# Layer two's norm folded into its matrices, ScalarE evictions, products in steps, and edge lists made in node order in a two-layer graph kernel

## The chip, the cores and the metric

The kernel runs on one core of a Trainium2 chip. The core has a matrix engine (TensorE, PE in the profile, with its weight loads as PEld), three engines for elementwise work (VectorE or DVE, ScalarE or ACT, GpSimd or POOL), a queue engine (SyncE or SP) and 16 DMA engines. Each engine runs its instructions in order, and they wait for each other through semaphores. Data lies in device memory (DRAM) or in on-chip memory of 128 partitions (SBUF), and matrix products land in PSUM. The metric is the device time of one execution in microseconds; lower is better.

## What is computed

There are N = 1250 nodes with 768 features, E = 20000 edges (source, destination, one of 34 types), sorted by destination. The reference, cut to what matters:

```
h   = relu(layernorm(x))
# layer one, 8 heads of 96; layer two, one head of 768
def gatv2(x, src, dst, Ws, bs, Wd, bd, attn):
    fs = x @ Ws + bs;  fd = x @ Wd + bd
    e  = leaky_relu(fs[src] + fd[dst], 0.2)
    logits = sum(e * attn)                       # per head
    alpha  = softmax of logits over the edges of a destination
    return elu(segment_sum(alpha * fs[src], dst))
g   = layernorm(gatv2(h, ..., W1s, b1s, W1d, b1d, attn1) + h) * ln1_w + ln1_b
o   = layernorm(gatv2(g, ..., Wos, bos, Wod, bod, attno)) * lno_w + lno_b
x   = x + o;  h = relu(layernorm(x))
# relational stage: mean of h over the edges of each type, times that type's 768 x 768 matrix
h1  = sum over r of mean_r(h[src]) @ W_rel[r] + h @ W_root + b_rgcn
out = x + normalised neighbour sum of (h1 @ W_gcn) + b_gcn
```

Everything is computed in 32-bit floats. A second path (`general_path`) stands behind a flag for inputs that don't fit the fast path's limits, and is not run here.

## The kernel before, in words

Nodes are ranked by in-degree and laid out as NT = 10 tiles of 128 nodes in that order. All nodes of tile k have at most CAPS[k] incoming edges (33, 22, 20, 18, 17, 16, 15, 14, 13, 11; 179 in all), so layer one and layer two each walk over 179 *slots*: slot s of tile k is the s-th incoming edge of each of the tile's 128 nodes.

**Front (`fast_front`, L627).** It loads the edges, x and layer one's weights, normalises x row by row (`h0`, also written to DRAM), turns it into columns, and finds for each node where its edges start and how many there are. From these come a key (L843 to L861: products into `wide`, copied to `keys`), the rank (ten passes of VectorE, L865), and a scatter of (node, first edge, degree) into `rank_d` in rank order (L880). The ranked record is read back (L901), and only then the edges of each ranked node are gathered as windows of 64 (L912) and shifted into place (L916 to L930). `sources(j)` (L807) computes node tile j of layer one's table `fs_d`: 26 products, two ScalarE copies, a store. Two of its ten calls stand between the steps of the ranking; `tc.issue_after` fixes that order on TensorE.

**Pair lists (`pairs`, L937, called from `prepare_lists`, L1349).** They give each edge its place in the lists by which the relational stage gathers. VectorE does nearly all of it, and three prefix sums go over TensorE (L966 to L983). The places are written to DRAM and read back (L1069, L1375), the lists are filled with default entries (L1354 to L1373), and each edge is then scattered into them, one indirect DMA for each slot.

**Layers one and two (`attention`, L1172).** The slots of a tile are cut into one or two chunks of at most CHUNK = 20. `front(c, i)` (L1194) issues for a slot an indirect gather of 128 rows of the table into `fs`, a ring of 24 buffers, and gives VectorE the logits: a maximum with the tile's negated destination rows (L1208), a product with the attention vector and a sum (L1213 and L1214 in layer one, L1210 in layer two). `softmax(c)` (L1217) turns a chunk's logits into weights. `back(c, i)` (L1250) scales the rows, on ScalarE by heads in layer one (L1266), and sums them on TensorE (L1268, L1258) into PSUM; the ring buffer is free after that. The loop at L1323 runs `back` of a chunk beside `front` of the next.

- `begin` (L1306) prepares the next tile's negated destination rows in the middle of a chunk. In layer one, `negated1` (L1409) gathers the tile's `h0` rows, makes columns and multiplies by W1d; VectorE evicts and applies the bias (L1416).
- `end` (L1282) closes a tile behind the loop over the chunk: shares, ELU, then `finish1` (L1420) or `finish2` (L1459). `finish1` adds h0, normalises, applies `lnw` and `lnb` (L1426, L1427), makes columns, multiplies by Wos, evicts with the bias (L1433), forms a further column of the table (L1435), scatters the 769 columns to layer two's table, multiplies by Wod and evicts the negated rows (L1440). Each product is one run of 24 instructions (`dense`, L1111).
- `list_edges` (L1385) puts the edge scatters into GpSimd's queue: 0.9 for each slot from slot 20 on, and 60, that is all the rest, behind layer one's last gather.

The products of a tile's start and end share one PSUM buffer (tag `mm2`) and one column buffer (`hT1`). The order on each engine is made by a planner that takes instructions by their place in the program and by a modelled time; `tc.issue_after(ins)` holds instructions of one engine behind `ins`.

**Relational stage and output (L1527, L1625).** 139 products of gathered tiles with the types' matrices, then the neighbour sums.

## Time and profile before

| | us |
|---|---|
| median of four runs | 2764.71 (2760.81 to 2769.98) |
| profiled execution, device time | 2764.21 |
| its span, first to last instruction | 2762.4 |
| first gather of layer one's rows | 154.3 |
| first scaling of gathered rows in layer one (L1266) | 246.7 |
| last gather of layer one | 794.1 |
| first gather of layer two | 886.5 |
| first load of a type's matrix | 1358.0 |
| granted TensorE clock, mean | 0.933 |

In the profile a row names the line of the program, the engine, the operation, what is written and what is read, how many instructions the row stands for, and in brackets how long the engine had been idle and what ended that. In a table by stage, busy times of the engines stand with the number of instructions in parentheses, then the granted clock, the share of the DMA engines and the rate in GB/s. A wait is given as total time, number of times and longest one. L1148 and L1152 are the helpers for indirect gathers and scatters, so their rows are told apart by what they write and read.

### The profile page before, as it was taken

Reading aid. Unit: us, or ns where it says so; the run is one execution under the profiler, and the core shown is the slowest. Engines: PE = TensorE matmul, PEld = TensorE weight load, DVE = VectorE, ACT = ScalarE, POOL = GpSimd, SP = SyncE. Lnnn points to the kernel's source line nnn. Section 1 sums busy time; section 2 is a strip of 40 time slices with the busy share of each in tenths; the row PEclk is TensorE's granted clock in tenths of the full one; section 3 lists DMA queues with packets and bytes.
Section 4 is the critical chain, followed back from the end, with each engine's and each line's share of the span. In section 5 each row is a group of like instructions: output and inputs, shape, how many; then the busy total and the mean of one; then the engine's idle time right before and its main releaser. Section 6 shows DMA issues by size and latency. Waiting matters only on the chain. (4 is left out here: it accounts for less than half of the span.)

```text
span 2762.4 us, 24188 instructions
## 1 busy us (share of the span) xinstructions
PE 2356.7 (85%) x7759; PEld 1366.4 (49%) x7759; DVE 1564.4 (57%) x2361; ACT 853.6 (31%) x2308; POOL 1525.2 (55%) x1113
## 2 busy tenths in 40 slices
PE   5953685789997486988699999999999999999688
PEld 3531252445454243544356666666666666666254
DVE  5599979998994999999262222222223222210262
ACT  3004765767862132333211121211211212212010
POOL 1343877777884775876275444444445454431471
PEclk9976897999999698999899999999999999999899
DMA  6155443445431776775477777777777777766783
GB/s 211 46 166 178 133 133 98 127 133 140 134 102 65 261 213 184 223 220 166 154 232 197 191 186 192 193 198 195 189 190 188 186 195 194 175 165 151 215 266 119
DMA packets 136548, 476.85 MB, mean 173 GB/s; under 512 B 26185, under 2 KB 28514, under 8 KB 136413
## 3 DMA queue, kind: packets, MB, share of 16 engines
q0 software_dynamic: 83712, 334.44, 46.7%
q1 hardware_dynamic: 48043, 134.21, 13.7%
q10 hardware_dynamic: 4658, 6.57, 0.7%
q8 instruction: 64, 1.05, 0.2%
q14 instruction: 71, 0.58, 0.1%
HBM read 385.91 MB, written 89.33 MB: 172 GB/s over the span
## 5 line engine op out<-in xcount | busy, mean ns | idle before, releaser
L1116 PE MATMUL ps<-wrel,mT 128*128 128x384 f32 x3336 | 1099.8, 486 | 1.0 <-DMA wrel<-in_L_gnn_W_rel_dram 1.0
L1116 PEld LDWEIGHTS ps<-wrel,mT 128*128 128x128 f32 x3336 | 623.5, 190 | 407.3 <-issue 1.4
L1148 POOL DMA_INDIRECT g<-r_h_d,lists x241 | 340.2, 1412 | 525.8 <-DVE g L1580 288.8
L1268 PE MATMUL ag<-fs,identf 128*128 128x384 f32 x716 | 288.4, 535 | 156.6 <-ACT fs L1266 146.9
L1580 DVE TENSOR_TENSOR g<-g,g 128x768 f32<-128x768 f32 x68 | 64.5, 949 | 614.8 <-DMA g<-r_h_d,lists 364.4
L1208 DVE TENSOR_TENSOR z<-fs,nfd 128x776 f32<-128x776 f32 (+1 forms) x358 | 347.5, 987 | 42.2 <-DMA fs<-f_fs_d,rec 21.2
L1266 ACT ACTIVATE fs<-fs,lg 128x96 f32<-128x96 f32 x1376 | 370.0, 363 | 0.3
L1258 PE MATMUL ag<-fs,dg 128*128 128x384 f32 x716 | 249.9, 510 | 82.6 <-ACT dg L1256 82.6
L1148 POOL DMA_INDIRECT fs<-f_fs_d,rec x179 | 247.3, 1382 | 97.4 <-issue 50.3
L1152 POOL DMA_INDIRECT r_pair_d<-rec,place x179 | 238.0, 1330 | 85.0 <-issue 43.9
L1603 POOL DMA_INDIRECT r_h_d<-y,lists x139 | 224.0, 1612 | 110.1 <-ACT y L1602 52.7
L1148 POOL DMA_INDIRECT fs<-r_fs_d,rec x179 | 239.4, 1337 | 81.1 <-issue 31.0
L1268 PEld LDWEIGHTS ag<-fs,identf 128*128 128x128 f32 x716 | 133.4, 202 | 298.4 <-ACT fs L1266 240.5
L1258 PEld LDWEIGHTS ag<-fs,dg 128*128 128x128 f32 x716 | 140.9, 200 | 188.5 <-ACT dg L1256 89.7
L1602 ACT ACTIVATE y<-ps,lists 128x768 f32<-128x768 f32 x71 | 64.1, 902 | 479.4 <-PE ps L1116 479.4
L1602 ACT ACTIVATE y<-ps,rcnt 128x768 f32<-128x768 f32 x68 | 61.4, 902 | 455.5 <-PE ps L1116 455.5
L1210 DVE SCALAR_TENSOR_TENSOR z<-z,attn_o 128x769 f32<-128x769 f32 x179 | 175.0, 995 | 0.6 <-ACT dg L1256 0.5
L1665 DVE TENSOR_TENSOR acc<-acc,nb 128x768 f32<-128x768 f32 x69 | 66.1, 958 | 187.0 <-DMA nb<-r_h_d,srcz 185.9
L1213 DVE TENSOR_TENSOR z<-z,attn 128x776 f32<-128x776 f32 x179 | 168.2, 954 | 0.1
L1214 DVE TENSOR_REDUCE lg<-z 128x8 f32<-128x776 f32 x179 | 167.8, 949 | 0.1
L1513 DVE SCALAR_TENSOR_TENSOR arow<-node,from_f,arow 128x1250 f16<-128x1250 f16 x110 | 166.2, 1511 | 1.7
L1104 PEld LDWEIGHTS pt<-identf,g 128*128 128x128 f32 x834 | 100.4, 142 | 54.6 <-issue 24.0
(283 smaller groups left out, 2314.3 us busy)
## 6 DMA issues: line engine op xcount, KB each, us to landing
wrel<-in_L_gnn_W_rel_dram SPq DMA_DIRECT2D x37, 2304.0 KB
g<-r_h_d,lists POOLq DMA_INDIRECT x241, 4.9
r_nfd_d<-fd SPq DMA_DIRECT2D x10, 384.0 KB
nfd<-r_nfd_d SPq DMA_DIRECT2D x10, 384.0 KB
r_x_d<-xb SPq DMA_DIRECT2D x10, 384.0 KB
x1r<-r_x_d SPq DMA_DIRECT2D x10, 384.0 KB
f_fs_d<-o_s SPq DMA_DIRECT2D x9, 388.0 KB
x<-in_x_dram SPq DMA_DIRECT2D x9, 384.0 KB
```

The costliest lines, as they stand in the source:

```text
L1116: last = nc.tensor.matmul(ps[:n, half, :f.HW], hT[:, k, j * P:j * P + n], w[:, k, cols], start=(k == 0), stop=(k == f.KC - 1 and not bias))
L1148: return nc.gpsimd.indirect_dma_start(out=to, out_offset=None, in_=table, in_offset=bass.IndirectOffsetOnAxis(ap=idx, axis=0))
L1152: s = nc.gpsimd.indirect_dma_start(out=table, out_offset=bass.IndirectOffsetOnAxis(ap=idx, axis=0), in_=rows, in_offset=None, **kw)
L1208: nc.vector.tensor_tensor(z, fs, t.nfd, op=ALU.max)
L1210: nc.vector.scalar_tensor_tensor(z[:, 0, :], z[:, 0, :], 1.0, attn_e[:, 0, :], op0=ALU.mult, op1=ALU.mult, accum_out=t.lg[:, s, :])
L1213: nc.vector.tensor_mul(z, z, attn_e)
L1214: nc.vector.tensor_reduce(t.lg[:, s, :], z, axis=AX.X, op=ALU.add)
L1258: nc.tensor.matmul(c.ps[:, half, :HW], dg, fs[:, 0, half * HW:(half + 1) * HW], start=begin, stop=end)
L1266: nc.scalar.activation(fs[:, h, :HD], fs[:, h, :HD], AF.Copy, scale=t.lg[:, s, h:h + 1])
L1268: nc.tensor.matmul(c.ps[:, half, :HW].rearrange("p (h d) -> p h d", d=HD), f.identf, fs[:, half * H // 2:(half + 1) * H // 2, :HD], start= ...
L1513: nc.vector.scalar_tensor_tensor(a, node16, from_f[:, k, s:s + 1], a, op0=ALU.is_equal, op1=ALU.add)
L1603: s = nc.gpsimd.indirect_dma_start(out=h1_d[:, :], out_offset=bass.IndirectOffsetOnAxis(ap=j.node, axis=0), in_=y, in_offset=None, compute ...
```

## The change

It has four parts.

*Front.* The edge windows are gathered and shifted in node order, before and beside the ranking, and the record that is scattered by rank carries a node's 33 edges with it (35 words instead of 4). None of the `sources` calls stands ahead of the ranking's products any more; all ten follow `last_keys`. The lists' default entries and zero rows are written in the front. `place` stays on the chip. Biases of layer one's destination rows are one row that a product with `ones_row` adds.

*Norm folded.* `ln1_w` is multiplied into Wos and Wod (`fold`, six ScalarE scalings each), `ln1_b` and the biases become one row for Wod and one row `bias_s`, which is added to layer two's weighted sums in `share`. The table's further column becomes a 769th column of Wos. Nodes without incoming edges are masked by `has`.

*Steps.* A tile's end and start return lists of steps: a transposition of three blocks, or six instructions of a product (half of one half). They go to `todo`, and the loop over a chunk runs them, spread evenly behind its slots. A tile with one chunk is closed two slots into the next chunk. ScalarE evicts each half of a product. For the last two tiles the product with Wos comes first, and that with Wod after both.

*Lists.* 30 edge scatters go behind gather 24 of tile 0, then 0.85 for each slot, 4 behind the last gather, and the rest behind the table scatters of tiles 7 and 8.

```diff
-    rank_d = dram.tile([NP, 4], I32, name="f_rank_d")
+    rank_d = dram.tile([NP, 2 + S0], I32, name="f_rank_d")
...
+    f.place = keepp.tile([P, NT, S0], I32, name="place")
+    f.h2_d = dram.tile([NP + P, D], F32, name="r_h2_d")
+    f.ZERO = NP + (PT + 1) * P
+    f.h1_d = dram.tile([f.ZERO + 1, D], F32, name="r_h1_d")
+    f.pair_d = dram.tile([P * COLS, 3], I32, name="r_pair_d")
...
+        f.bias_1 = const.tile([1, D], F32, name="bias_1")
+        nc.scalar.dma_start(f.bias_1, bass.AP(tensor=b1d.tensor, offset=b1d.offset, ap=[[0, 1], [1, D]]))
+        f.bias_s = const.tile([P, D], F32, name="bias_s")
...
+        fill = prep.tile([P, COLS, 3], I32, name="fill")
+        nc.vector.memset(fill[:, :, 2], 0)
...
+        nc.sync.dma_start(f.pair_d.rearrange("(p c) f -> p c f", p=P), fill)
+        zero = prep.tile([P, D], F32, name="zero")
+        nc.vector.memset(zero, 0.0)
+        nc.sync.dma_start(f.h2_d[NP:, :], zero)
+        for t in range(PT + 1):
+            nc.sync.dma_start(f.h1_d[NP + t * P:NP + (t + 1) * P, :], zero)
+        nc.sync.dma_start(f.h1_d[f.ZERO:, :], zero[:1])
...
-        last = sources(0)
...
-        with tc.issue_after(last.ins):
-            last = nc.tensor.matmul(sh_ps[:, 0:1], shift, first[:, 0:1], start=True, stop=True)
-        with tc.issue_after(last.ins):
-            last = sources(1)
+        nc.tensor.matmul(sh_ps[:, 0:1], shift, first[:, 0:1], start=True, stop=True)
...
+        win = prep.tile([P, NT, WIN], I32, name="win")
+        for j in range(NT):
+            nc.gpsimd.indirect_dma_start(
+                out=win[:EP, j, :], out_offset=None, in_=win_d[:, :],
+                in_offset=bass.IndirectOffsetOnAxis(ap=arow[:EP, j:j + 1], axis=0))
...
+        wf = prep.tile([P, NT, WIN], F32, name="wf")
+        nc.vector.tensor_copy(wf[:EP], win[:EP])
...
+        rec = prep.tile([P, NT, 2 + S0], I32, name="rec")
         nc.vector.tensor_copy(rec[:, :, 0], node)
-        nc.vector.tensor_copy(rec[:, :, 1], first[:, :NT])
-        nc.vector.tensor_copy(rec[:, :, 2], deg)
-
-        past = prep.tile([NP - N, 4], I32, name="past")
+        nc.vector.tensor_copy(rec[:, :, 1], deg)
+        nc.vector.tensor_copy(rec[:EP, :, 2:], wf[:EP, :, :S0])
...
-            sources(2)
+            sources(0)
...
-        for j in range(3, NT):
+            nc.vector.scalar_tensor_tensor(f.place, pad, float(P * COLS), pl, op0=ALU.mult, op1=ALU.add)
+
+        for j in range(1, NT):
...
-            if s >= CHUNK or t.k:
+            if t.k == 0 and s == ring - 1:
+                list_edges(row, 30)
+            elif t.k or s >= ring:
                 list_edges(row, rate)
             if t.k == NT - 1 and s == t.S - 1:
                 list_edges(row, rest)
+                f.last_row = row
...
+            if bias is not None:
+                nc.vector.scalar_tensor_tensor(halves(o, P, f), ps[:, :, :HW], by, halves(bias, P, f),
+                                               op0=ALU.mult, op1=ALU.add)
...
-            for i in range(max(now.n, after.n if after else 0)):
-                if i < now.n and after:
+            steps = max(now.n, after.n if after else 0)
+            for i in range(steps if after else 0):
+                if i < now.n:
                     back(now, i)
-                if after and i < after.n:
+                if i < after.n:
                     front(after, i)
-                if i == now.n // 2:
+                if i == 1:
+                    while ended:
+                        critical, rest_of = end(ended.pop())
+                        todo.extend(critical + rest_of)
                     begin(j + 2)
+                for at, what in extra:
+                    if at == (j, i):
+                        todo.extend(what())
+                if i:
+                    run(-(-len(todo) // (steps - i)))
...
-                end(now.t)
+                if j + 2 < len(chunks) and len(now.t.done) == 1:
+                    ended.append(now.t)
+                else:
+                    critical, rest_of = end(now.t)
+                    if j + 2 < len(chunks):
+                        todo.extend(critical + rest_of)
+                    else:
+                        for step in critical:
+                            step()
+                        later += rest_of
+        for step in later:
+            step()
...
+    f.has = rp.tile([P, NT], F32, name="has")
+    nc.vector.tensor_scalar(f.has, f.degf, 0.5, None, op0=ALU.is_gt)
...
+        def fold(i):
+
+            wos, (cols, rows, sums) = late["wos"], late["made"]
+            w = (wos, late["wod"])[i]
+            held = {}
+
+            def bias(half):
+                if half == 0:
+                    held["ps"] = ps_t.tile([P, 2, 512], F32, name="b_ps", tag="mm2")
+                ps, at = held["ps"], slice(half * HW, (half + 1) * HW)
+                for k in range(KC):
+                    nc.tensor.matmul(ps[:1, half, :HW], cols[:, 1, k:k + 1], w[:, k, at], start=(k == 0), stop=False)
+                if i:
+                    nc.tensor.matmul(ps[:1, half, :HW], f.ones_row[:, :1], sums[:, 0, at], start=False, stop=False)
+                nc.tensor.matmul(ps[:1, half, :HW], f.ones_row[:, :1], rows[:, i, at], start=False, stop=True)
+                if half:
+                    nc.scalar.copy(sums[:, i, :].rearrange("p (a b) -> p a b", a=2), ps[:1, :, :HW])
+
+            def scaled(k):
+                nc.scalar.activation(w[:, k, :D], w[:, k, :D], AF.Copy, scale=cols[:, 0, k:k + 1])
+
+            def spread():
+                ps = ps_t.tile([P, 2, 512], F32, name="b_ps", tag="mm2")
+                for half in range(2):
+                    nc.tensor.matmul(ps[:, half, :HW], f.ones_row, sums[:, 0, half * HW:(half + 1) * HW], start=True, stop=True)
+                nc.scalar.copy(halves(f.bias_s, P, f), ps[:, :, :HW])
+
+            def quarters(k):
+                wt = work.tile([P, D], F32, name="wt2", tag="att_e")
+                nc.vector.scalar_tensor_tensor(wt, wos[:, k, :D], SLOPE / (1.0 - SLOPE), f.attn_o[:, 0, :D],
+                                               op0=ALU.mult, op1=ALU.mult, accum_out=wos[:, k, D:])
+
+            steps = [lambda h=h: bias(h) for h in range(2)] + [lambda k=k: scaled(k) for k in range(KC)]
+            if i == 0:
+                steps += [spread] + [lambda k=k: quarters(k) for k in range(KC)]
+            return steps
+
+        def product(hT, w, width, bias, evict):
+
+            held = {}
+
+            def step(half, part):
+                if (half, part) == (0, 0):
+                    held["ps"] = ps_t.tile([P, 2, 512], F32, name="ps", tag="mm2")
+                at = slice(half * HW, (half + 1) * HW if half == 0 else width)
+                ps = held["ps"][:, half, :at.stop - at.start]
+                for k in range(3 * part, 3 * part + 3):
+                    nc.tensor.matmul(ps, hT[:, k], w[:, k, at], start=(k == 0), stop=(k == KC - 1 and bias is None))
+                if part:
+                    if bias is not None:
+                        nc.tensor.matmul(ps, f.ones_row, bias[:, at], start=False, stop=True)
+                    evict(ps, half, at)
+
+            return [lambda h=h, p=p: step(h, p) for h in range(2) for p in range(2)]
+
+        def columns(hT, row, both):
+
+            def step(g):
+                pt = ps_t.tile([P, 512], F32, name="pt", tag=f"ptc{g}")
+                for c in range(3):
+                    nc.tensor.transpose(pt[:, c * P:(c + 1) * P], row[:, (g + c) * P:(g + c + 1) * P], f.identf)
+                copy = nc.scalar.copy if both or g == 0 else nc.vector.tensor_copy
+                copy(hT[:, g:g + 3, :], pt[:, :3 * P].rearrange("p (c n) -> p c n", c=3))
+
+            return [lambda: step(0), lambda: step(3)]
...
+            def evict(ps, half, at):
+                nc.scalar.activation(nfd[:, half * H // 2:(half + 1) * H // 2, :], ps.rearrange("p (h d) -> p h d", d=D // H),
+                                     AF.Copy, scale=-1.0)
+
+            return columns(hT, h0s[k], True) + product(hT, f.w1d, D, f.bias_1, evict)
...
-            nc.vector.tensor_mul(o, o, lnw)
-            nc.vector.tensor_add(o, o, lnb)
-            hT = pool.tile([P, KC, P], F32, name="hT1", tag="hT1", bufs=1)
-            to_columns(nc, ps_t, f, hT, 0, o, P)
-            ps = dense(nc, ps_t, f, hT, wos, 0, P, tag="mm2")
-            ap1 = late["pool"]
-            fs = ap1.tile([P, W2], F32, name="fs2", tag="fs2", bufs=1)
-            nc.vector.tensor_add(halves(fs, P, f), ps[:, :, :HW], halves(bias_s, P, f))
-            wt = work.tile([P, D], F32, name="wt2", tag="att_e")
-            nc.vector.scalar_tensor_tensor(wt, fs[:, :D], SLOPE / (1.0 - SLOPE), attn_o, op0=ALU.mult, op1=ALU.mult,
-                                           accum_out=fs[:, D:])
-            scatter(fs2_d[:, :], fs, f.perm[:, k:k + 1], "fs2")
-            ps = dense(nc, ps_t, f, hT, wod, 0, P, tag="mm2")
-            fd = ap1.tile([P, D], F32, name="fd2", tag="fd2", bufs=1)
-            nc.vector.scalar_tensor_tensor(halves(fd, P, f), ps[:, :, :HW], -1.0, halves(bias_d, P, f),
-                                           op0=ALU.mult, op1=ALU.subtract)
-            nc.sync.dma_start(nfd2_d[k * P:(k + 1) * P, :], fd)
-
-        attention(H, f.fs_d, negated1, f.attn_1, prepare_lists, loads1, finish1, 0.9, 60)
+            if k < NT - 2:
+                hT = pool.tile([P, KC, P], F32, name="hT1", tag="hT1", bufs=1)
+            else:
+                hT = pool.tile([P, RW], F32, name="hT1r", tag="fs", bufs=24)[:, :D].rearrange("p (k n) -> p k n", k=KC)
+            held = {}
+
+            def to_table(ps, half, at):
+                if half == 0:
+                    held["fs"] = ap1.tile([P, W2], F32, name="fs2", tag="fs2", bufs=1)
+                nc.scalar.copy(held["fs"][:, at], ps)
+                if half:
+                    row = scatter(fs2_d[:, :], held["fs"], f.perm[:, k:k + 1], "fs2")
+                    if NT - 4 < k < NT - 1:
+                        list_edges(row, 7 if k < NT - 2 else 40)
+
+            def negative(ps, half, at):
+                if half == 0:
+                    held["fd"] = ap1.tile([P, D], F32, name="fd2", tag="fd2", bufs=1)
+                nc.scalar.activation(held["fd"][:, at], ps, AF.Copy, scale=-1.0)
+                if half:
+                    nc.sync.dma_start(nfd2_d[k * P:(k + 1) * P, :], held["fd"])
+
+            return columns(hT, o, False) + product(hT, wos, W2, None, to_table), product(hT, wod, D, late["bias_d"], negative)
+
+        attention(H, f.fs_d, negated1, f.attn_1, prepare_lists, loads1, finish1, 0.85, 4,
+                  extra=(((0, 5), lambda: fold(0)), ((1, 2), lambda: fold(1))))
...
+            for a in (sc, sh):
+                nc.vector.tensor_mul(a, a, f.has[:, k:k + 1])
...
+            return [], [lambda: root(k, hT)]
+
+        def root(k, hT):
...
```

## The prediction

> **What bounds the kernel now.** I read the page first (which engine is full in which stretch), then busy time by stage, then VectorE's waits in layer one, then single rows of the timeline where the stages meet.
>
> From the page:
>
> ```profile
> PE 2356.7 (85%) x7759; PEld 1366.4 (49%) x7759; DVE 1564.4 (57%) x2361; ACT 853.6 (31%) x2308; POOL 1525.2 (55%) x1113
> PE   5953685789997486988699999999999999999688
> DVE  5599979998994999999262222222223222210262
> POOL 1343877777884775876275444444445454431471
> ```
>
> Slices are 69 us. TensorE is full only from slice 21 on, in the relational stage, which the diff does not touch. The slices before it are VectorE's and GpSimd's, and all edits lie there. Busy time by stage, in the order PE, PEld, DVE, ACT, POOL, clock, DMA:
>
> ```profile
> 246.00:400.00 154.00, 121.28 (x307) 55.48 (x308) 131.43 (x185) 125.28 (x456) 119.60 (x90) 0.89 0.46 128
> 400.00:600.00 200.00, 134.03 (x402) 74.51 (x401) 187.50 (x251) 117.94 (x406) 155.41 (x102) 0.85 0.41 115
> 600.00:824.00 224.00, 206.99 (x625) 114.02 (x624) 207.91 (x289) 166.08 (x561) 176.03 (x135) 0.96 0.45 128
> 824.00:887.00 63.00, 53.35 (x161) 30.65 (x160) 28.16 (x49) 18.02 (x44) 26.47 (x25) 0.95 0.09 32
> 887.00:1358.00 471.00, 362.13 (x1063) 200.74 (x1061) 423.22 (x808) 141.00 (x282) 316.95 (x228) 0.89 0.63 198
> 1372.00:2560.00 1188.00, 1173.13 (x4220) 722.76 (x4220) 324.30 (x287) 238.46 (x467) 562.49 (x380) 0.99 0.74 190
> ```
>
> In layer one (246 to 824) VectorE is 91% busy. GpSimd looks lighter, but each of its 327 instructions there is followed by a gap of 0.30 us, which adds 98 us to its 451: 549 of 578 us, 95%. TensorE reaches 92% after 600. Three engines are close to full, so removing work from one soon meets the next. What VectorE waits for from 184 to 824:
>
> ```profile
> DVE z L1208 <- DMA fs<-f_fs_d,rec: 21.2, 18, 4.4
> DVE nfd L1416 <- PE ps L1116: 15.4, 4, 8.2
> DVE fd L1440 <- PE ps L1116: 6.8, 2, 6.1
> ```
>
> 27 us (with 2.7 and 2.3 us for L1433 and L1108) come from products lumped at a tile's end, 21 us from gathered rows that are late. The timeline, start and duration:
>
> ```profile
> 369.52 0.98 POOL L1148 DMA_INDIRECT fs<-f_fs_d,rec  x1 [0.30 <-issue]
> 411.21 2.29 POOL L1148 DMA_INDIRECT fs<-f_fs_d,rec  x1 [0.30 <-issue]
> 794.09 2.31 POOL L1148 DMA_INDIRECT fs<-f_fs_d,rec  x1 [0.30 <-issue]
> 856.59 0.96 DVE L1433 TENSOR_TENSOR fs<-ps,bias_s 128x768 f32<-128x768 f32 x1 [10.42 <-DMA r_fs_d<-fs,f_perm]
> 858.47 0.55 DVE L1291 TENSOR_SCALAR att_e<-att_o 128x768 f32<-128x768 f32 x1
> 882.63 0.95 POOL L1152 DMA_INDIRECT r_fs_d<-fs,f_perm  x1 [22.77 <-DVE wt L1435]
> 886.53 0.98 POOL L1148 DMA_INDIRECT fs<-r_fs_d,rec  x1 [2.95 <-DMA r_fs_d<-fs,f_perm]
> ```
>
> A gather takes 0.98 us beside an idle VectorE and 2.29 beside a full one. Layer two can't start before the last tile's table rows are scattered (882.6), 58 us after layer one's last slot (824.3).
>
> **The sum** is against the profiled execution: 2764.2 us, span 2762.4, 0.5 us under the median 2764.7. A measurement of this kernel can tell about 0.2% (5.5 us) from no change.
>
> **Front, -4 us.** Two `sources` tiles leave the path to the ranks: the key products move from 67.6 to about 56, ranks end at 74 instead of 85.6. The window gathers (10 x 1.25 us of POOL) go beside the ranking; their alignment (119.5 to 129.5) follows it, the ten scatters take 15 us, and edge lists exist near 105 instead of 130. But `sources` now starts at 56 instead of 36: ten tiles of 9.9 us end at 155 instead of 148.4, so the rows that layer one gathers come 7 us later, and the pair list's prefix products (148.3 to 155.3, queued behind `sources`) end at 162. VectorE turned to their results only at 163.2, busy with L1027 to L1030 (16 us), which now fit in before: gain 1. The fill work (216.1 to 218.5) moves to 50 to 100, where VectorE is 39% busy, and the first negated row's eviction (0.96) goes to ScalarE. 1 + 2.5 + 1 = 4. The seven fill stores (2.7 MB) move past the SP queue's `h0` stores into the first 50 us, whose DMA rate is 283 GB/s: up to 9.5 us if they delay the weights, nothing if they follow the loads, as program order has it; I take nothing. The reload of `place` through DRAM (2 us) was hidden. Bounds: -10 (prefix products slip between `sources`) to +9.5.
>
> **Layer one, VectorE.** Gone per tile: L1416, L1426, L1427, L1433, L1435, L1440, 0.95 us each. Between 246 and 794 (last gather) that is 9 + 4x7 + 7 = 44 instructions, 42 us; added are six `quarters`, 5.7. Of 497.7 us busy, 461 stay.
>
> **ScalarE** takes 60 half evictions (0.43 a step, from the 0.48 us hT copies), 12 scalings at 0.9 (L1602's 0.90) and three copies at 0.8: 40 us more on 409 of 578: 78%. Behind each eviction in its queue stand the scalings that release `fs`; a step waits at most for one product half. Hidden by the 22% left; if not, 40 us over ten tiles.
>
> **TensorE.** Per tile now: three products at 7.9 (x24), two transposes of 0.9; new: four bias rows at 0.84 (L814, 0.91 us for two passes). 28.9 us a tile instead of 25.5, plus 1.3 a slot. The folds add 23 us (four rows of about 5.4, two of 0.84), from tile 0's second chunk on, where TensorE is 79% busy. Their first step, near 255, waits for `wos`; the layer's weights came at 396 to 414 GB/s between 230 and 247, now from about 210 and without five broadcast rows (1.9 MB), so it does not wait; if it did, the slots' products behind it would wait as long, and with them the ring. Spreading removes the 27 us of waits; what is late next is the rows. With the steps move the table scatter (POOL, one 0.98 us issue among some 15 gathers of the next chunk) and the store of the negated rows (SP, ahead of layer two's loads of the same rows); nobody reads either before layer two, except for tiles 8 and 9, below.
>
> **GpSimd.** Its count does not fall. Before: 307 instructions from 246 to 794, 37 edge scatters left. After: 30 edges in one go behind gather 24, 0.85 per slot instead of 0.9, four at the end, the rest behind tiles 7 and 8. The 30 start when the list is there (before: 221; after: some 206), in time that was idle (25.7 us waiting for ring slots), so about 25 are out by 242; 143 edges, 154 gathers and 16 others make 313 until the last gather. Price: 1.29 us (0.98 + 0.30) beside an idle VectorE, and 497.7 / (307 - 50.3/1.29) = 1.86 beside a busy one. With some 475 us of VectorE work in that time (the 461, and part of the 30 us by which it trailed GpSimd at the end): T = 475 + 1.29 x (313 - 475/1.86) = 549 us. From 242 the last gather is issued at 791, 3 earlier than now.
>
> The Trainium skill, "GPSIMD Engine Reference", section "Key points", says that GpSimd contends with VectorE instructions that read two SBUF tensors. The 2.29 against 0.98 us fits. By it only L1426, L1427 and L1435 of the removed six weigh on GpSimd, the others read one operand from PSUM; as an estimate from that page, 21 us of relief instead of 42 up to the last gather, 21 x (1 - 1.29/1.86) = 6 us less gained, and a sum of -36 instead of -42.
>
> **Layer change, -39 us.** Paced by GpSimd, the last slot follows its gather in some 9 us (landing 4.6, z 2.6) instead of 30: 800. Behind it, before: 58 us to the scatter. Tile 9's ELU stood in VectorE's order behind tile 8's eviction (858.47; its sum was there at 843.8): 14.6. L1426 and L1427 go (2), and eviction with L1435 (2.2) becomes 0.5: 18 in all, less one for the half bias-free column and a scatter that can wait behind the last 6 edges. 17 gained: layer two's first gather at 845 instead of 886.5. So -42 with the front: -4, -38 or so here.
>
> **Layer two, 0.** L1274 becomes a three-operand form: 0.95 (L1433) for 1.008. Two 0.15 us multiplies a tile: 3. The tile end moves two slots back; `root` is one step of 10 us as before. VectorE is 97% busy from 900 to 1300. Bounds -8 to +5. The relational stage and the rest: nothing.
>
> **Rivals.**
> 1. *GpSimd starves layer one (slower).* Place: the burst and the 313 instructions. From 403 to 437 it got 15 through in 35 us, 2.33 each, beside back-to-back slots. At 2.33 instead of 1.86, T = 475 + 1.29 x (313 - 204) = 616: +25, 2790. It decides from 2.12 on, where layer two starts at 886 again. For it: 400 to 600 ran at 1.96. Against it: a starved VectorE idles, and rows then cost 1.29. Chance 0.15.
> 2. *GpSimd keeps up, TensorE or VectorE bounds.* From 438 to 788 TensorE needs 100 slots x 1.3 + 6 x 28.9 = 304 us; at 95% 320 instead of 350: -30. From 246 to 438 the waits go: -20. With front and 17: -71, -65 with the quarters: 2699. For it: 600 to 794 ran at 1.73. Chance 0.24.
> 3. *The waits only change places* (steps of 2 us hold up the slots' products, ring slots come late): 2762. For it: TensorE's 92% after 600. Chance 0.08.
>
> Forecast: 2764.2 - 42 = **2722**, chance 0.53, own range 2704 to 2745.
>
> **How the numbers follow.** Rival 2 spreads from 2677 to 2712; below 2690 about 0.08. Rival 1 lies above 2768 with about 0.12. Range 2690 to 2768. Faster: 0.53 + 0.24 + 0.02 = 0.79; same 0.06; slower 0.15.
>
> **What would show it.** Front: key products near 56, `sources` end near 155, first softmax near 242. Layer one: no PE waits on VectorE's nfd, fd; z waits on gathered rows growing to 60 to 80 us; last gather near 791. First gather of layer two near 845; layer two 470 us long. Wrong if GpSimd's mean price beside a busy VectorE leaves 1.75 to 2.0, if the fill stores delay the first weights, or if ScalarE's evictions hold TensorE's single product buffer.

## The result, and the profile after

The changed kernel takes 2768.93 us (median), the kernel before 2766.54 us in the same sets of runs: a ratio of 1.0014, interval 1.0007 to 1.0021. It is slower by 0.14%, less than the 0.2% that the prediction calls a difference. Predicted were 2722 us, in a range from 2690 to 2768.

The profiled execution of the changed kernel took 2773.55 us, its span is 2771.7. That is 4.6 us above its median, and the kernel before was profiled 2.3 us below its own: the spans compared here differ by 9.3 us, the medians by 2.4. The milestones, in us from the start of the span:

| | before | after | difference | predicted |
|---|---|---|---|---|
| first gather of layer one's rows | 154.3 | 179.4 | +25.1 | +7 |
| first scaling (layer one's `back` begins) | 246.7 | 267.3 | +20.6 | -4 |
| last gather of layer one | 794.1 | 810.7 | +16.6 | -3 |
| sum of tile 9 (`att_o`) | 842.8 | 865.2 | +22.4 | -24 (its last slot) |
| first gather of layer two | 886.5 | 891.8 | +5.3 | -42 |
| first load of a type's matrix | 1358.0 | 1365.8 | +7.8 | -42 |

So the front lost 20.6 us, layer one gave 4.0, the layer change 11.3, and layer two took 2.5 more. From the page:

```profile
PE 2416.5 (87%) x7903; PEld 1380.0 (50%) x7903; DVE 1516.1 (55%) x2323; ACT 891.8 (32%) x2383; POOL 1534.0 (55%) x1113
PE   3876685999999486898699999999999999999687
DVE  7658869989785999999262222222232222210262
POOL 3237777777654776786275444444454454431471
```

VectorE lost 48 us of work and TensorE got 60 more. VectorE's digits in slices 3 to 13, mostly 9 before, now run from 5 to 9. Busy time by stage (PE, PEld, DVE, ACT, POOL, clock, DMA):

```profile
267.00:403.00 136.00, 99.32 (x241) 41.84 (x242) 112.90 (x167) 115.87 (x415) 106.18 (x87) 0.89 0.45 121
403.00:600.00 197.00, 154.65 (x458) 82.06 (x457) 167.95 (x221) 125.76 (x433) 153.01 (x104) 0.90 0.44 124
600.00:811.00 211.00, 200.80 (x598) 107.57 (x597) 176.07 (x246) 163.31 (x540) 148.95 (x121) 0.97 0.49 140
811.00:865.00 54.00, 52.01 (x159) 28.52 (x158) 45.30 (x67) 39.71 (x125) 18.59 (x14) 1.00 0.10 30
```

From the first scaling to the last gather VectorE is 84% busy instead of 91%. What it waits for in that time (line, total, times, longest):

```profile
DVE att_o L1300 <- PE ag L1289: 28.1, 4, 9.1
DVE att_e L1300 <- PE ag L1289: 18.4, 1, 18.4
DVE z L1229 <- DMA fs<-f_fs_d,rec: 16.3, 9, 5.1
DVE z L1229 <- ACT nfd L1521: 11.8, 3, 7.4
DVE den L1255 <- ACT lg L1253: 6.9, 7, 4.2
```

The waits for products, L1416, L1433 and L1440, are gone (24 us from 246 to 794). In their place stand 46.5 us for TensorE's sums, which cost nothing in this stretch before, and 11.8 us for negated rows. VectorE's idle time rose from 50 to 87 us (548 less 498 busy before, 544 less 457 after), which uses up all but 4 of the 41 us of removed work.

**Where the front lost.** TensorE and ScalarE between 80 and 120 us, in the timeline:

```profile
101.17 0.91 PE L841 MATMUL ps<-bias,ones_row 1*128 1x388 f32 x2
111.99 6.05 PE L840 MATMUL ps<-w1s,hT 128*128 128x388 f32 x12 [9.90 <-ACT o_s L845]
110.87 0.30 ACT L1407 ACTIVATE dinv<-f_degf,f_ones_col 128x10 f32<-128x10 f32 x1 [27.68 <-DVE f_degf L953]
```

ScalarE's queue stands before a 0.30 us square root that needs the ranked record. Behind it wait the copies of `sources`, and TensorE has no free PSUM buffer for 9.90 us. Then it restarts at a low clock (granted 0.68 from 112 to 118, 1.00 from 118 to 124): 6.05 us for twelve matmuls that take 4.18 when it runs on. (The Trainium skill, "TensorE: Matmul & The Clock Gate", section "Part 1: The HAM clock gate", says that the clock falls after an idle window of about 3.4 us; these rows agree.)

The kernel before has the same square root in this queue, and there it did no harm:

```profile
104.90 0.30 ACT L1377 ACTIVATE dinv<-f_degf,f_ones_col 128x10 f32<-128x10 f32 x1 [14.88 <-DVE f_degf L904]
```

It stood behind four copies of `sources`, not two, and the ranked record came 6 us earlier (read from 104.5 on, now from 110.5 on). The record is late although the ranking's first pass starts at 60.9 instead of 70.1: among the ten passes in VectorE's queue now stands the conversion of the edge windows, which waits for their gathers,

```profile
73.71 0.49 DVE L915 CAST wf<-win 125x640 f32<-125x640 int32 x1 [6.65 <-issue]
```

so that the ranks end at 85.4 as before, and the scatter by rank now waits for the shifted edges too (first at 91.6 instead of 86.1).

The second loss is at the first softmax:

```profile
238.53 5.78 PE L1457 MATMUL b_ps<-wos,ln_cols 128*1 128x384 f32 x12 [14.41 <-DMA ln_cols<-in_L_gnn_ln_b_dram]
256.01 0.28 DVE L1252 TENSOR_TENSOR lg<-lg,mx 128x128 f32<-128x128 f32 x1
262.34 2.58 ACT L1465 ACTIVATE wod<-wod,ln_cols 128x768 f32<-128x768 f32 x3 [9.16 <-PE b_ps L1457]
266.24 0.31 ACT L1253 ACTIVATE lg<-lg 128x128 f32<-128x128 f32 x1
```

The logits are ready at 256.3, but the Exp (L1253) starts 10 us later. Ahead of it in ScalarE's queue are scalings of Wod, which wait for `fold`'s products, which waited until 238.5 for the columns of `ln1_b`.

**Where layer one gave nothing.** The change from tile 1 to tile 2, VectorE first:

```profile
390.12 0.31 DVE L1255 TENSOR_REDUCE den<-lg 128x8 f32<-128x88 f32 x1 [4.17 <-ACT lg L1253]
410.00 0.96 DVE L1300 TENSOR_TENSOR att_e<-ag,old 128x768 f32<-128x768 f32 x1 [18.43 <-PE ag L1289]
401.02 4.03 PE L1493 MATMUL ps<-f_w1d,hT 128*128 128x384 f32 x12
412.77 0.49 ACT L1521 ACTIVATE nfd<-ps 128x384 f32<-128x384 f32 x1 [0.26 <-PE ps L1496]
```

VectorE does next to nothing from 386 to 413. It has finished its slots and needs two things: the sums of the chunk, which share TensorE with the spread steps, and tile 2's negated rows (`nfd`), whose steps come last in the list and end at 413.

**The tail.** Rows of TensorE and VectorE behind the last gather (810.7):

```profile
843.97 4.04 PE L1493 MATMUL ps<-wod,hT 128*128 128x384 f32 x12
848.78 16.39 PE L1289 MATMUL ag<-fs,identf 128*128 128x384 f32 x50
865.21 0.96 DVE L1300 TENSOR_TENSOR att_o<-ag,den 128x768 f32<-128x768 f32 x1 [3.68 <-PE ag L1289]
```

Products of tile 7 with Wod stand ahead of the last sums. VectorE is late too: it waited for tile 7's sum until 809.9, and only from 813.3 on took tile 9's eleven slots, the last of which ended at 844.8, 34 us behind its gather.

### The profile page after: what moved, and what is told of

It reads as the page before. It is cut to its first block, busy times and chain, and to the rows that moved or that the text cites. A ratio compares the mean times of both kernels' runs of the same rounds, so it can differ in the third digit from the quotient of the medians.

```text
span 2771.7 us, 24487 instructions
## 1 busy us (share of the span) xinstructions
PE 2416.5 (87%) x7903; PEld 1380.0 (50%) x7903; DVE 1516.1 (55%) x2323; ACT 891.8 (32%) x2383; POOL 1534.0 (55%) x1113
## 5 line engine op out<-in xcount | busy, mean ns | idle before, releaser
L1165 POOL DMA_INDIRECT fs<-f_fs_d,rec x179 | 239.2, 1336 | 89.4 <-issue 36.3
L1124 PEld LDWEIGHTS pt<-identf,g 128*128 128x128 f32 x834 | 100.4, 142 | 54.9 <-issue 24.0
```

What stands on the lines that cost most here:

```text
L1165: return nc.gpsimd.indirect_dma_start(out=to, out_offset=None, in_=table, in_offset=bass.IndirectOffsetOnAxis(ap=idx, axis=0))
```

## The experiments

All numbers are in us. "Front" is the first scaling, "layer" the time from there to the last gather, "change" the time from there to the first gather of layer two. The ratio is to the kernel before, measured in the same set of runs.

| run | edits | ratio | interval | front | layer | change |
|---|---|---|---|---|---|---|
| before | | 1 | | 246.7 | 547.4 | 92.4 |
| after | | 1.0014 | 1.0007 to 1.0021 | 267.3 | 543.4 | 81.1 |
| e1 | sources early | 0.9962 | 0.9947 to 0.9977 | 253.2 | 535.8 | 82.3 |
| e2 | root late | 0.9966 | 0.9953 to 0.9980 | 255.6 | 543.3 | 81.3 |
| e6 | old front | 0.9966 | 0.9950 to 0.9981 | 252.4 | 539.2 | 82.4 |
| e3 | no edges | one run | | 265.9 | 527.2 | 81.8 |
| e4 | start first | 0.9950 | 0.9932 to 0.9969 | 270.3 | 519.1 | 80.7 |
| e5 | e4, no bias rows | 0.9925 | 0.9898 to 0.9952 | 266.9 | 522.9 | 77.3 |
| e7 | e1 + e2 + e4 | 0.9888 | 0.9862 to 0.9914 | 249.8 | 525.4 | 80.3 |
| e8 | e7, late product | 0.9923 | 0.9896 to 0.9951 | 244.9 | 561.1 | 54.9 |
| e9 | Exp first | 1.0035 | 1.0014 to 1.0056 | 258.3 | 574.7 | 84.6 |
| e10 | e7 + e9 | 0.9872 | 0.9843 to 0.9901 | 234.7 | 552.7 | 78.5 |
| e11 | e10, late product | 0.9859 | 0.9830 to 0.9889 | 236.8 | 552.7 | 70.3 |
| e12 | e11, both copies | 0.9840 | 0.9817 to 0.9862 | 238.8 | 551.3 | 68.4 |
| e16 | e12 again | 0.9908 | 0.9888 to 0.9928 | 234.8 | 549.7 | 68.9 |
| e13 | e12, short burst | 0.9830 | 0.9809 to 0.9851 | 241.4 | 533.6 | 68.9 |
| e14 | e9, short burst | 0.9969 | 0.9956 to 0.9981 | 255.8 | 537.3 | 81.2 |
| e15 | short burst | 1.0006 | 0.9994 to 1.0017 | 269.5 | 532.1 | 82.9 |

Runs e9 to e12 form one set, on a chip on which the kernel before took 2788.47 us; in the other three sets it took 2765.7 to 2768.6. The six edits took 2744.00 us there and 2738.65 elsewhere, so the kernel before suffers more from that chip. Ratios of that set are compared among themselves only, and a time of that set stands beside one of another only with this in mind.

The last three columns come from one execution of each kernel. Five kernels with one front (after, e3, e4, e5, e15) have the first scaling between 265.9 and 270.3, e7 and e8 with one front have 249.8 and 244.9, and e12 and e16, the same kernel, have layers of 551.3 and 549.7: a difference below some 5 us in these columns decides nothing.

### The front: e1, e2, e6

e1, the order of `sources` as before:

```diff
+        last = sources(0)
         gotf = prep.tile([P, NT, RW], F32, name="gotf")
...
+        with tc.issue_after(last.ins):
+            last = nc.tensor.matmul(sh_ps[:, 0:1], shift, first[:, 0:1], start=True, stop=True)
+        with tc.issue_after(last.ins):
+            last = sources(1)
```

> The changed kernel with the three `sources` tiles back where the kernel before had them (0 and 1 around the ranking's first product, 2 behind the key products). Theory A (layer one starts 20.6 us later because all ten `sources` tiles start at 60 instead of 36 and TensorE then idles): the last copy of `sources` falls from 173 to 150 to 160, the first gather from 179 to 155 to 166, the first scaling of layer one from 267 to 245 to 254, and the whole run is 13 to 22 us faster than the changed kernel. Rival B (VectorE's pair-list work paces the front, `sources` only lies beside it): first gather earlier, first scaling still above 262, run within 5 us of the changed kernel.

e2, the square root for `dinv` behind the last copy:

```diff
-        nc.scalar.activation(f.dinv, f.degf, AF.Sqrt, bias=f.ones_col, scale=1.0)
+        with tc.issue_after(f.copied.ins):
+            nc.scalar.activation(f.dinv, f.degf, AF.Sqrt, bias=f.ones_col, scale=1.0)
```

> The changed kernel with the square root for `dinv`, which waits for the ranked record, held behind the last copy of `sources` on ScalarE. Theory A (ScalarE's queue, stopped at that instruction from 83 to 110.9, stops the copies and so TensorE for 9.9 us, and TensorE then starts at a cold clock for 1.9): the idle 9.9 us on TensorE before 112 is gone, the last copy of `sources` is at 161 to 163 instead of 173, the first scaling at 255 to 258 instead of 267, the run 9 to 12 us faster. Rival B (the front is paced by VectorE): TensorE's idle time goes, the first scaling moves less than 3 us.

Theory A held in both (e2's last copy came 1.4 us later than expected). The last copy of `sources` came at 159.9 and 164.4 instead of 174.0, the first scaling 14.1 and 11.7 us earlier, and against the changed kernel the runs are 0.5% faster (0.9962 and 0.9966 over 1.0014). The two gains are partly the same time: in e1 the square root still stops TensorE, for 5.39 us instead of 9.90. e6 puts the whole front of the kernel before under the rest of the change (its `fast_front`, fill work behind `pairs`, reload of `place`):

> The changed kernel with the whole front of the kernel before (ranking, windows after the ranked record, fill work and the reload of `place` behind the pair lists); fold, steps, evictions and the order of the edge scatters stay changed. Theory A (the new front alone costs the 20.6 us by which layer one starts later): first scaling at 243 to 251, first gather of layer two at 868 to 876, the run 16 to 24 us faster than the changed kernel and about 0.6 to 0.8% faster than the kernel before. Rival G (what the late front costs is hidden, layer one's end is set elsewhere): first scaling early, but the run within 6 us of the changed kernel.

The first scaling came at 252.4 and the run is 0.5%, some 13 us, faster than the changed kernel, 0.34% faster than the kernel before. That is below the 16 expected: with the old front the first scaling is still 5.7 us later than in the kernel before. Its trace shows the logits ready at 244.1 and the Exp at 251.5, behind `fold`'s scalings again (e9). And since e1 and e6 agree within 1 us at the first scaling, the rest of the new front neither gained nor cost there.

### What paces layer one: e3, e5, e4

e3 leaves all edge scatters out:

```diff
-    edges = [(k, s) for k in range(NT) for s in range(CAPS[k])]
+    edges = []
```

> The changed kernel without the 179 edge scatters into the pair lists (so the relational stage gathers default rows: only layer one is read). From first scaling to last gather the changed kernel takes 543 us. Theory P, the prediction's (GpSimd paces layer one): with 170 instead of 313 GpSimd instructions it is no longer full, VectorE's 475 us with small gaps remain, 475 to 490 us. Rival C (GpSimd isn't the pace; VectorE waits for TensorE's sums and negated rows, TensorE and ScalarE are the pace): only the 16 us of waits for gathered rows can go, 527 to 543 us.

527.2 us in the one run: theory P, the prediction's, falls. The groups of GpSimd in layer one (busy, mean ns, then its idle time):

```profile
L1165 POOL DMA_INDIRECT fs<-f_fs_d,rec x154 | 218.5, 1419 | 282.2 <-PE ag L1289 214.8 <-ACT fs L1287 32.9 <-issue 12.7
```

With 143 instructions fewer, GpSimd waits 215 us for TensorE to release ring buffers. VectorE keeps its waits for sums (45.9) and negated rows (12.5) and loses only those for rows (16.3 to 2.3).

e4, the start's steps ahead of the closing tile's, one line in `start_tile`:

```diff
-            todo.extend(negated(k, t.nfd[:, :, :HD]))
+            todo[0:0] = negated(k, t.nfd[:, :, :HD])
```

> The changed kernel with the steps of a tile's start (transposes, product with W1d, eviction of the negated rows) put ahead of the closing tile's steps in the list, not behind them. Theory D (the negated rows come last in a chunk, so VectorE stands still at each change of tile until they are there: 6 to 10 us for each of some seven tiles): the waits of VectorE at the tile changes (nfd 12, sums 46 us) fall below 30, first scaling to last gather falls from 543 to 505 to 525, the run is 15 to 35 us faster. Rival E (TensorE's work, 95% busy from 600 on, is the pace whatever the order): first scaling to last gather within 8 us of 543, the run within 8 us.

519.1 us instead of 543.4: theory D held, by order alone and with the same work. VectorE's waits from 270 to 789:

```profile
DVE z L1229 <- DMA fs<-f_fs_d,rec: 23.5, 23, 2.5
DVE den L1255 <- ACT lg L1253: 14.7, 2, 9.3
DVE hT L1508 <- PE pt L1506: 12.4, 3, 6.1
```

The waits for sums are gone from this stretch; with the tail, up to 870, they are 25.4 us instead of 50.1. e5 takes TensorE's four bias products per tile out of e4:

```diff
-            return columns(hT, h0s[k], True) + product(hT, f.w1d, D, f.bias_1, evict)
+            return columns(hT, h0s[k], True) + product(hT, f.w1d, D, None, evict)
...
-        return ..., product(hT, wod, D, late["bias_d"], negative)
+        return ..., product(hT, wod, D, None, negative)
```

> The kernel with the start's steps first, without the bias rows on TensorE in layer one (the four products of ones_row for each tile, 3.4 us; the biases of W1d and Wod are left out of the result). From first scaling to the last tile's sum (att_o of tile 9) the kernel with the start first takes 571.9 us. Theory E (TensorE is full from 600 on and in the tail, 52.8 of 53 us): each us of its work there is one on the path, 547 to 560 us, and the run 10 to 25 us faster than with the rows. Rival F (VectorE and the gathered rows are the pace, TensorE only follows closely): 567 us or more, the run within 5 us.

From the first scaling to tile 9's sum it takes 572.5 us, with the rows 571.9. Rival F held: TensorE's 95% from 600 on did not make its load the pace. The run is 0.25% faster than e4, some 7 us where rival F allowed 5, but the intervals of the two overlap; 3.4 us stand in the front, which the edit does not touch, and 3.4 in the layer change. From 270 to 870 TensorE only waits more for scalings, 52.0 us instead of 31.0:

```profile
PE ag L1289 <- ACT fs L1287: 52.0, 28, 29.8
```

### Edits together, and the tail: e7, e8

> The changed kernel with three edits together: `sources` in its old places, the square root behind the last copy, the start's steps first. One at a time they gave -14 and -12 us at the first scaling and -24 us in layer one. If the two front edits take away different time (theory A: late start, and stop of ScalarE's queue): last copy of `sources` at 148 to 152, first scaling at 241 to 246, first gather of layer two at 843 to 850, the run 2724 to 2734 us. Rival H (they meet a common bound, VectorE's pair-list work in the front, gathered rows in layer one): first scaling above 248 or layer one above 530, the run 2738 us or more.

2737.61 us is rival H's time but for 0.4, and the first scaling at 249.8 is its sign; the last copy of `sources` at 154.3 and the first gather of layer two at 855.5 also miss theory A. Neither of H's causes shows, though: layer one took 525.4, and the logits were there at 236.8 and the Exp started at 248.75, again behind `fold`. That led to e9.

e8 moves tile 7's Wod product behind the last table scatter, with its columns in a ring buffer:

```diff
-                        critical, rest_of = end(ended.pop())
-                        todo.extend(critical + rest_of)
+                        t = ended.pop()
+                        critical, rest_of = end(t)
+                        if H > 1 and t.k >= NT - 3:
+                            todo.extend(critical)
+                            later.extend(rest_of)
...
-            if k < NT - 2:
+            if k < NT - 3:
```

> The three edits, and tile 7's product with Wod (8.7 us with its bias rows) moved from the tail of layer one behind the last tile's table scatter, where those of tiles 8 and 9 are. Theory E (TensorE is full from the last gather to the last sum): the sum of tile 9 and the first gather of layer two come 7 to 10 us earlier than with the three edits alone, and the run is as much faster. Rival F (the tail follows VectorE and ScalarE): less than 3 us.

The run became slower than e7. GpSimd's queue, in the timeline:

```profile
791.58 0.98 POOL L1174 DMA_INDIRECT r_fs_d<-fs,f_perm  x1 [14.29 <-ACT fs L1551]
804.67 0.99 POOL L1170 DMA_INDIRECT fs<-f_fs_d,rec  x1 [0.30 <-issue]
805.96 0.97 POOL L1170 DMA_INDIRECT fs<-f_fs_d,rec  x1 [0.31 <-issue]
```

The last two gathers stand behind tile 7's table scatter, which waits 14.3 us for its eviction, and behind seven edge scatters. e11, which has e9's edit besides, makes the same move without the ring buffer and doesn't show it, which points to the ring buffer; whether the gathers waited for that buffer itself, or the planner took another order because of it, was not told apart.

### Fold and the burst: e9, e15, e14

e9 holds ScalarE's part of `fold` behind the first softmax:

```diff
...
-                nc.scalar.activation(w[:, k, :D], w[:, k, :D], AF.Copy, scale=cols[:, 0, k:k + 1])
+                with tc.issue_after(f.exp.ins):
+                    nc.scalar.activation(w[:, k, :D], w[:, k, :D], AF.Copy, scale=cols[:, 0, k:k + 1])
```

> The changed kernel with one edit: ScalarE's work for `fold` (scalings of Wos and Wod, copy of the sums) held behind the Exp of layer one's first softmax. In the changed kernel the logits for that Exp are there at 256.3, but it starts at 266.2, behind scalings that wait for fold's products, which wait for the column load of ln1_b until 238.5. Theory I (fold in ScalarE's queue costs about half of the front's 20.6 us): first scaling at 257 to 259 instead of 267.3, run 6 to 10 us faster than the changed kernel. Rival J (held back, fold holds up TensorE's sums of the first slots instead): first scaling early, first scaling to last gather longer by as much, run within 4 us.

The first scaling came at 258.3, 9 us earlier, but the last gather at 833.0 instead of 810.7. The run took 2796.3 us, 27 more than the changed kernel, on the chip on which the kernel before takes 22 more; by the ratios (1.0035 against 1.0014, intervals that overlap) nothing was gained. VectorE and GpSimd:

```profile
293.54 0.97 DVE L1229 TENSOR_TENSOR z<-fs,nfd 128x776 f32<-128x776 f32 x1 [19.24 <-DMA fs<-f_fs_d,rec]
288.21 0.97 POOL L1169 DMA_INDIRECT r_pair_d<-rec,place  x1 [0.30 <-issue]
289.49 0.99 POOL L1165 DMA_INDIRECT fs<-f_fs_d,rec  x1 [0.30 <-issue]
```

This wait is not `fold`'s on TensorE (rival J's mechanism) but the burst's: the 25th gather stands behind the 30 edge scatters. It is not the only one that grew: VectorE's waits for the Exp rose from 6.9 to 17.0 us and those for negated rows from 11.8 to 16.7. With the short burst, in e14, they are back at 6.7 and 11.7. e15 shortens the burst alone, e14 does both:

```diff
-                list_edges(row, 30)
+                list_edges(row, 6)
...
-                        list_edges(row, 7 if k < NT - 2 else 40)
+                        list_edges(row, 17 if k < NT - 2 else 40)
...
-        attention(H, f.fs_d, negated1, f.attn_1, prepare_lists, loads1, finish1, 0.85, 4,
+        attention(H, f.fs_d, negated1, f.attn_1, prepare_lists, loads1, finish1, 0.85, 18,
```

> The changed kernel with the short burst alone. Theory M: the Exp still starts at 266, ring slots come free only from 268 on, and the burst of 30 was through at 285; of the 7.3 us that VectorE waited for rows from 267 to 403, at most that is gained: the run 0 to 7 us faster than the changed kernel. Rival O (the burst alone is the cost, fold's hold-up is harmless): 12 us or more.

> The changed kernel with two edits: Exp ahead of fold's scalings, and the short burst of 6 edge scatters. The first alone gave nothing: first scaling 9 us earlier, then 19.2 us of waiting for rows behind the burst. Theory M (fold's hold-up of the Exp and the burst of 30 cover each other): first scaling at 257 to 259, the wait for rows near 293 below 4 us, the run 8 to 16 us (0.3 to 0.6%) faster than the changed kernel, whose ratio to the kernel before was 1.0014. Rival N: within 4 us of the changed kernel.

Alone the short burst brings 2 us at most (1.0006 against 1.0014, intervals that overlap), together with the Exp 12 us (0.9969); the longest wait for layer one's rows in e14 is 2.2 us. Theory M held: the two delays lie side by side, and each hides the other. (In e15 the layer alone is 11 us shorter, of which the medians show little; with one execution of each this stays open.)

### The rest: e10, e11, e12, e16, e13

> The three edits (`sources` in old places, square root late, start first) and the Exp ahead of fold's scalings. With three, the first softmax's logits were there at 236.8, Exp started at 248.8. Theory I: first scaling at 238 to 240 instead of 249.8, first gather of layer two at 843 to 848 instead of 855.5, run 7 to 12 us faster than with three (2737.6). Rival J: run within 4 us of it.

e10 is e7 with e9's edit. Its stages went as e9's: the first scaling is 15 us earlier than in e7, layer one 27 longer, with the same wait of 19.2 behind the burst. Its 2752.9 us are 15 more than e7's, again on the chip on which the kernel before takes 22 more, so the run itself decides neither for theory I nor for rival J.

e11 is e10 with e8's move, but without its last hunk (the columns keep the buffer `hT1`):

> The four edits, and tile 7's product with Wod moved behind the last table scatter; its columns stay in their own buffer this time (the first try took a ring buffer, and the gathers of the last tile waited for it: last gather 806 instead of 775). Theory E (TensorE is full from the last gather to the last sum, 54.8 of 55 us): last gather to first gather of layer two falls from 80 to 69 to 74 us, run 6 to 10 us faster than with four. Rival F (the tail follows VectorE and ScalarE): less than 3 us.

Last gather to first gather of layer two fell from 78.5 to 70.3: in the tail, unlike before it, TensorE's work is the path (theory E). The run gained 0.13%, some 4 us, less than the 6 to 10 expected, with intervals that overlap. From the last gather to the sum of tile 9 it is 42.5 us instead of 52.6.

e12 is e11 with both column copies of a closing tile on ScalarE:

```diff
-            return columns(hT, o, False) + product(hT, wos, W2, None, to_table), ...
+            return columns(hT, o, True) + product(hT, wos, W2, None, to_table), ...
```

> The five edits, and both column copies of a closing tile on ScalarE (with three edits VectorE, in order, stood 23 us in front of its copy of the second three columns, waiting for TensorE's transposes and ScalarE's queue). Theory K (in-order waits of VectorE at the tile's end are what is left of layer one): first scaling to last gather 8 to 20 us shorter than with five edits, run as much faster. Rival L (ScalarE is 80 to 93% busy there and passes the wait on: the copies hold up the scalings): within 4 us, or slower.

> The six edits once more, so that the seventh is compared on one chip: a ratio of 0.982 to 0.986 to the kernel before.

VectorE's waits in front of its own copy are gone, layer one is 1.4 us shorter instead of 8 to 20, and the run 5 us faster, with intervals that overlap: near rival L. The waits came back as late rows:

```profile
DVE z L1234 <- DMA fs<-f_fs_d,rec: 62.7, 32, 19.3
```

e16 gave 0.9908, not 0.982 to 0.986, because the kernel before was faster on that chip. e13 adds the short burst:

> The six edits, and the edge scatters spread otherwise: 6 instead of 30 behind gather 24 of tile 0, 18 instead of 4 behind the last gather, 17 instead of 7 behind tile 7's table scatter (there GpSimd stood still for 19 and 15 us). With six edits VectorE waits 19.3 us at 274 for rows whose gather stands in GpSimd's queue behind that burst. Theory M (the burst takes the place of the front's lost time): that wait falls below 4 us, the last gather comes 10 to 20 us earlier after the first scaling (551 us with six edits), the run is 0.4 to 0.7% faster than six edits on the same chip. Rival N (the rows are late in any case, GpSimd's 313 instructions pace layer one): the wait moves to later slots, first scaling to last gather stays within 5 us, the run within 4 us.

```profile
DVE z L1234 <- DMA fs<-f_fs_d,rec: 46.1, 31, 4.3
DVE z L1234 <- ACT nfd L1533: 6.9, 2, 3.7
```

The wait of 19.3 is gone, layer one is 16 us shorter than in e16 on the same chip, and the run 0.8% faster by the medians, more than the 0.4 to 0.7 expected. (The profiled execution, at 2731.2 us the slowest of five, is only 6.7 us faster than e16's, since its first scaling is 6.6 later.) Rows that come late remain VectorE's largest wait. No run leaves out the edges in this kernel, so whether GpSimd paces it is open. At 2720.20 us e13 beats both kernels: 0.983 of the kernel before (0.9809 to 0.9851), some 46 us.

## Why the prediction was wrong, point by point

- **Front, -4: measured +20.6.** The step that failed first is "`sources` now starts at 56 instead of 36: ten tiles of 9.9 us end at 155". They started at 60.3 and the last copy was at 174. Four us are the later start, two the first product at a low clock (6.3 for 4.2, granted 0.67 from 60 to 67), twelve the stop behind `dinv`'s square root and the restart. I had counted the tiles and not asked what else stands in ScalarE's queue. e2 gives 12 us back, e1 14. The key products came in time (55.6 to 60.1), but the ranks did not end at 74: they ended at 85.4, the same as before, because the conversion of the windows stood among their passes for 6.65 us. (The gain's terms, 1 + 2.5 + 1, add up to 4.5, not 4.)
- **Fold "does not wait".** The step looked at `wos` alone; the wait was for the columns of `ln1_b`. And the work behind it that counted was not the slots' products on TensorE, as the step said, but the Exp on ScalarE: 10 of the 20.6 us by the rows, 9 by e9, 5.7 with the old front (e6). That e14 gains 12 us fits.
- **The burst "in time that was idle".** It started at 225, not at 206, and kept GpSimd until 282: its first eight scatters took 21 us beside a full VectorE, 2.6 each, where I had counted 25 of 30 out by 242. In the changed kernel it lay beside `fold`'s delay (e15: 2 us at most); without that delay VectorE waits 19 us behind it (e9, e16), and the short burst brings 18 us (e13 against e16).
- **VectorE, 36 us less: right.** From the first scaling to the last gather it is 457 us instead of 498, in 544 instead of 548.
- **GpSimd paces layer one, 549 us: the number right, the reason wrong.** Measured 543.4. By the prediction's own formula the price beside a busy VectorE is 457 / (310 - 87/1.29) = 1.88, within the bounds it set. (From 400 to 600 before, that formula gives 2.03; the prediction's 1.96 is the plain mean, 200/102.) But the formula assumes that GpSimd never waits for others; it waited 46 us for ring buffers, and e3, without the edges, still needed 527. That the number was met is luck. The sign it gave, waits for rows growing from 21 to "60 to 80 us", did not come: they fell to 16.3. Only with the six edits, when the other waits are gone, are they 62.7. The reading "549 of 578 us, 95%" was an occupancy, not a path. The same holds for TensorE's 95% (e5). What held this kernel was the order in the queues: e4 takes 24 us off without less work.
- **ScalarE "hidden by the 22% left", spreading that "removes the 27 us of waits": failed.** The waits for products went, and 46.5 us for sums came, since products and evictions now stand among the slots' sums and scalings, and the rows needed first were computed last. That was rival 3, "the waits only change places", to which I gave 0.08 and 2762 us. It named the mechanism; its time lacked the front.
- **Layer change, -39: measured -11.3.** Of its terms, 17 for tile 9's end was right: from its sum to the table scatter it takes 22.0 instead of 39.8. "The last slot follows its gather in some 9 us" failed: it took 34, four more than before, since VectorE had waited for tile 7's sum. From the last gather to the last sum it is 54.5 us instead of 48.7, and TensorE is full there (52 of 54 us), with tile 7's products among the rest. e11 removes 8 us of it.
- **Layer two 0, relational stage 0:** +2.5, within the bounds given, and within 2 us. Not examined.
- **The skill's rule.** "GPSIMD Engine Reference", section "Key points", says that GpSimd contends with VectorE instructions with two SBUF operands: gathers in layer one took 1.35 us in the mean instead of 1.42, but since GpSimd was not the path in the changed kernel, no run here decides between 36 and 42 us.

## What to carry to other kernels

An engine that is 95% busy is not yet the path: leave its work out and see (e3, e5), before a gain is worked out from its count. When work moves to another engine, write down what stands behind it in that engine's in-order queue and what it waits for; a 0.3 us instruction that waited for a late record stopped ScalarE for 27.7 us here and TensorE for 9.9, and had done no harm two copies further back. Of several steps spread behind a loop, put first what the next stage reads first, and when one fix gives nothing, look for the wait that had been lying beside it (e9 and e15 give nothing clear of the noise, e14 gives 12 us).

## What I had not expected of the hardware

- The load of two columns of 768 floats as single elements (`ln_cols`) was issued at 225.0 and 225.5 beside two matrices of 2.3 MB, and released TensorE only at 238.5, 13 us later. Whether the single elements or the neighbours made it slow was not tested.
- The same two kernels keep different distances on different chips: the kernel before 2788.5 against 2765.8 us (0.8%), the six edits 2744.0 against 2738.7 (0.2%). Why was not found.
